# A chunked retention block with a mixture of experts: the first step in another order, and transposes on VectorE through a DRAM copy from the eleventh chunk on

## The chip, the cores and the metric

The kernel runs on one core of a Trainium2 chip. The metric is the device time of one execution in microseconds; the kernel before has a median of 623.9 us in three runs (622.66 to 626.26). Durations and starts below come from one profiled execution of it.

## What is computed

The input x is [2, 2048, 256] in float32. A layernorm without scale, then a retention layer, and the result is added to x; a second layernorm, then a mixture of 8 experts of which each token takes 2, and this too is added. Cut to what matters here:

```python
y  = layernorm(x)
v  = y @ W_write.T                       # 4 heads of 64
wk = y shifted by one token              # the first one is zero
# chunk by chunk, with a state W per head:
inter = W @ rk * g_p                     # rk: the tokens y of the chunk
S     = rk @ wk.T ;  intra = (S * M) @ v
W     = g_C * W + (v * g_w).T @ wk
x1 = x + y + (alpha * (inter + intra)) @ W_read.T
out = x1 + sum over the top 2 of 8 experts of  p_e * (gelu(layernorm(x1) @ w1_e + b1_e) @ w2_e + b2_e)
```

M, g_p, g_w and g_C are powers of a decay gamma = sigmoid(decay), made at the start from its logarithm.

## The kernel before

**Tiling.** The 2048 positions are cut into 16 chunks (`p`, 0 to 15) of P = 128 tokens, and both batch rows (b = 0, 1) of a chunk are done together, so that a tile of tokens is 128 partitions x 2 x 256. Four groups of chunks are routed to the experts as they become ready. Routed tokens are gathered per expert into tiles of at most 256 tokens, and the expert work of a tile is cut into 8 `piece`s of 128 of the 1024 hidden units (L872): a matmul group `ph` (L894), the GELU on ScalarE to `hT` (L899), and three pieces later the matmuls `py` (L850). After the eighth piece VectorE makes `yo` (L861) and GpSimd adds the rows to the output in DRAM (L864).

**One chunk.** `norm_stats` (L286) takes mean and variance on VectorE; `rstd_of` (L243) raises the variance to the power -0.5 on GpSimd (L247). `norm` (L298) writes the normed tokens `y`: on VectorE for chunks 0, 1 and from 11 on, on ScalarE for the others. Still in `norm`, three DMAs make `wk`, which is y moved down by one partition: row 0 from the last row of the chunk before (L323), then 112 rows (L324) and 15 rows (L325). Then x of the chunk p+2 is asked for. `transposes` (L349) turns y into `yT` (features on partitions, with a column ahead for the token before): four TensorE transposes into the PSUM tile `pt` (L355), one copy out of it, on VectorE for chunk 0 (L358) and on ScalarE for the others (L361). `scaled_reads` (L364) multiplies yT by g_p to `rg`, `scaled_writes` (L373) multiplies wk by g_w to `wkg`, on ScalarE for chunks below 9 and on VectorE after (L382).

`attention(p)` (L418) is a generator; between its yields the main loop places pieces of the experts. In its order: the matmuls `pv` (v, L428), the scores `pS` (L437), the masked scores `A` on VectorE (L443), `scaled_writes(p)`, the output product of the chunk before (`result`, pO, L406), `transposes(p + 1)`, from chunk 9 on `norm_stats(p + 2)`, the gate (`gate_parts`, L340), then `pR` (L480, L488), its copy `rdT` (L493), `pW` (L508), the new `state` on VectorE (L513), `scaled_reads(p + 1)` and `norm(p + 2)`.

**What sets the order.** All five engines run in the order in which the code issues (`manual_schedule`, L101); no scheduler moves anything. Nearly all loads and stores go through SyncE's (SP's) one queue, among them the experts' weights `w1c` (1 MB each, L777), the gathered tokens `xg` (L791) and their extra columns `wn` (L797). A DMA that has to wait for its source holds back all that are issued behind it in that queue. The few loads that ScalarE issues are in the first lines (L111 to L115). PSUM tiles come from pools: tag `pm` has three buffers, which ph, pv, pW and the late pO take in turn; `ps_t` has one (pt), `ps_s` one (pS and pR), `ps_y` two. So a ph waits until the third `pm` tile ahead of it has been read. SBUF tiles with tag `y` have three buffers, `wk`, `yT` and `v` two.

**The first step.** L109 to L118 ask for x of chunk 0 in two halves (SP the first, ScalarE the second, after `dec`), the write weights and the gate weights. ScalarE makes |decay|, its exponential, alpha and the logarithm (L140 to L145). The generator `decays` (L147) is run in three parts by `next(start)`: `neg` (L149); then `lg` (L151), `g_w`, and on ScalarE the masks `dmask`, g_w, g_c and g_p; then on GpSimd the causal cut of `dmask` (L162). The start order stands at L918 to L933: warm-up matmuls, `norm_stats(0)`, `norm(0)`, the second part of `decays`, the correction of the gate weights in `wwg` (L927), `transposes(0)`, a part of the set-up, the third part of `decays`, `norm_stats(1)`, `norm(1)`.

**Constants.** EASY = 9: from this chunk on VectorE takes over some of ScalarE's work. BUSY = 8: from here on chunks run among the experts' pieces. The main loop is at L979.

Of the kernel before, what the change touches and what calls it, by code (L numbers as in the profile page):

```python
# [10 lines left out]
F32 = mybir.dt.float32  # L11
I32 = mybir.dt.int32
AF = mybir.ActivationFunctionType
ALU = mybir.AluOpType
# [4 lines left out]
P = 128  # L19
B, T, D = 2, 2048, 256  # L20
# [3 lines left out]
NC = T // P  # L24
# [6 lines left out]
S = 32  # L31
Q = P // S
# [28 lines left out]
def block_kernel(  # L61
# [12 lines left out]
    b2: bass.AP,  # L74
    out: bass.AP,
    slots: bass.AP,
):
    nc = tc.nc

# [2 lines left out]
    chk = ctx.enter_context(tc.tile_pool(name="chk", bufs=2))  # L82
# [7 lines left out]
    def one(shape, dt, name):  # L90
        return keep.tile(shape, dt, name=name)
# [4 lines left out]
    def load_x(p):  # L96
        xin = chk.tile([P, B, D], F32, tag="xin", name=f"xin_{p}", bufs=4)
        nc.sync.dma_start(xin, x.rearrange("b t d -> t b d")[p * P : (p + 1) * P])
        return xin
# [8 lines left out]
    wr_sb = one([P, 2, D], F32, "wr_sb")  # L108
    xins = {0: chk.tile([P, B, D], F32, tag="xin", name="xin_0", bufs=4)}  # L109
    nc.sync.dma_start(xins[0][:, 0, :], x[0, 0:P, :])  # L110
    nc.scalar.dma_start(dec, decay)  # L111
    nc.scalar.dma_start(xins[0][:, 1, :], x[1, 0:P, :])
    nc.sync.dma_start(wwg[:, :, :D], wwT.rearrange("(c p) o -> p c o", p=P))
    nc.scalar.dma_start(wwg[:, :, D:], gateT.rearrange("(c p) e -> p c e", p=P))
    nc.scalar.dma_start(lal, log_alpha)  # L115
# [25 lines left out]
    lg = one([P, 6], F32, "lg")  # L141
    nc.scalar.activation(lg, mag, AF.Exp, scale=-1.0)
    alpha = one([P, 2], F32, "alpha")
    nc.scalar.activation(alpha, lal, AF.Exp)
    nc.scalar.activation(lg, lg, AF.Ln, bias=1.0)  # L145

    def decays():  # L147

# [21 lines left out]
    g_w = one([P, H], F32, "g_w")  # L170
# [99 lines left out]
                return  # L270

    ys, wks, yTs, x1s, ups, stats2, rgs, wkgs = {}, {}, {}, {}, {}, {}, {}, {}
    shifts, vs, rdTs = {}, {}, {}
    EASY = 9
    BUSY = 8
    LATE = 7
    mark = {}
# [2 lines left out]
    def group_tiles(q):  # L280
        if q not in x1s:
            x1s[q] = grp.tile([P, G, D + E], F32, tag="x1", name=f"x1_{q}")
            stats2[q] = grp.tile([P, G, 2], F32, tag="mv2", name=f"mv2_{q}")
        return x1s[q], stats2[q]

    def norm_stats(p):  # L286
        xin = xins[p]
        st = sml.tile([P, B, 6], F32, tag="st", name=f"st_{p}")
        mv = sml.tile([P, B, 2], F32, tag="mv", name=f"mv_{p}", bufs=3)
        for b in range(B):  # L290
            nc.vector.bn_stats(st[:, b, :], xin[:, b, :])
        for b in range(B):
            beside()
            nc.vector.bn_aggr(mv[:, b, :], st[:, b, :])
        beside()
        ups[p] = (mv, *rstd_of(mv[:, :, 1], B, f"a{p}"))

    def norm(p):  # L298

        xin = xins[p]  # L300
        mv, ve, rstd = ups[p]
        shift = shift_of(mv[:, :, 0], rstd, B, f"a{p}")
        ups[p] = (mv, ve, rstd)
        beside()
        up = sml.tile([P, B], F32, tag="up", name=f"up_{p}")
        nc.vector.tensor_scalar(up, rstd, 1.0, None, ALU.add)
        shifts[p] = (shift, up)
        y = chk.tile([P, B, D], F32, tag="y", name=f"y_{p}", bufs=3)
        for b in range(B):
            if 1 < p < EASY + 2:  # L310
                nc.scalar.activation(
                    y[:, b, :], xin[:, b, :], AF.Identity, bias=shift[:, b : b + 1], scale=rstd[:, b : b + 1]
                )
            else:
                nc.vector.tensor_scalar(
                    y[:, b, :], xin[:, b, :], rstd[:, b : b + 1], shift[:, b : b + 1], ALU.mult, ALU.add
                )

        wk = chk.tile([P, B, D], F32, tag="wk", name=f"wk_{p}")
        if p == 0:  # L320
            nc.gpsimd.memset(wk[0:1, :, :], 0.0)
        else:
            nc.sync.dma_start(wk[0:1, :, :], ys[p - 1][127:128, :, :])  # L323
        nc.sync.dma_start(wk[1:113, :, :], y[0:112, :, :])  # L324
        nc.sync.dma_start(wk[113:128, :, :], y[112:127, :, :])  # L325
        ys[p], wks[p] = y, wk
        if p + 2 < NC:
            xins[p + 2] = load_x(p + 2)

    def sums(p):  # L330

# [17 lines left out]
    def transposes(p):  # L349

        yT = chk.tile([P, B, 2, P + 1], F32, tag="yT", name=f"yT_{p}")
        pt = ps_t.tile([P, B, 2, P], F32, tag="pt", name=f"pt_{p}")
        for b in range(B):
            for c in range(2):
                nc.tensor.transpose(pt[:, b, c, :], ys[p][:, b, c * P : (c + 1) * P], ident)  # L355
        if p == 0:
            nc.gpsimd.memset(yT[:, :, :, 0:1], 0.0)
            nc.vector.tensor_copy(yT[:, :, :, 1:], pt)  # L358
        else:
            nc.scalar.copy(yT[:, :, :, 0:1], yTs[p - 1][:, :, :, P : P + 1])  # L360
            nc.scalar.copy(yT[:, :, :, 1:], pt)  # L361
        yTs[p] = yT

    def scaled_reads(p):  # L364

# [7 lines left out]
    def scaled_writes(p):  # L373
        if p < NC - 1:
            wkg = chk.tile([P, B, H, HD], F32, tag="wkg", name=f"wkg_{p}", bufs=1)
            wk = wks[p].rearrange("p b (h d) -> p b h d", h=H)
            if p < EASY:
                for h in range(H):
                    nc.scalar.activation(wkg[:, :, h], wk[:, :, h], AF.Identity, scale=g_w[:, h : h + 1])
            else:  # L380
                for b in range(B):
                    nc.vector.tensor_tensor(  # L382
                        wkg[:, b], wk[:, b], g_w.unsqueeze(2).to_broadcast([P, H, HD]), ALU.mult
                    )
            wkgs[p] = wkg
# [32 lines left out]
    def attention(p):  # L418


        q, at = p // 2, 2 * (p % 2)
        first, last = p == 0, p == NC - 1
        x1, _ = group_tiles(q)
        yT = yTs[p]
        for b in range(B):
# [21 lines left out]
        beside()  # L447
        if p + 2 < NC and p < EASY:
            norm_stats(p + 2)
# [9 lines left out]
        if not last:  # L459
            transposes(p + 1)  # L460
        if p + 2 < NC and p >= EASY:
            norm_stats(p + 2)
# [11 lines left out]
        for b in range(B):  # L474
            if first:
                break
            for hh in range(2):
                for j in range(2):
# [3 lines left out]
                        start=(b == 0), stop=False,  # L482
                    )
        for b in range(B):
            for hh in range(2):
                for j in range(2):
                    hs = slice((2 * hh + j) * HD, (2 * hh + j + 1) * HD)
# [9 lines left out]
        for b in range(B):  # L497
            if p < EASY:
                nc.scalar.activation(x1[:, at + b, D:], vs[b][:, D:], AF.Identity, scale=std1[:, b : b + 1])
            else:  # L500
                nc.vector.tensor_scalar(x1[:, at + b, D:], vs[b][:, D:], std1[:, b : b + 1], None, ALU.mult)
        if not last:
            pW = ps_m.tile([P, B, 2, HD], F32, tag="pm", name=f"pW_{p}")
            for b in range(B):
                for hh in range(2):
                    for j in range(2):
                        h = 2 * hh + j
# [34 lines left out]
    def route(q):  # L542


        early = 2 * q + 2 < BUSY
        x1, mv2 = x1s[q], stats2[q]
# [363 lines left out]
    start = decays()  # L910
# [12 lines left out]
    norm_stats(0)  # L923
    next(start)
    norm(0)
    next(start)
    nc.vector.scalar_tensor_tensor(wwg[:, :, D:], by_e(ps, 2), -1.0 / D, wwg[:, :, D:], ALU.mult, ALU.add)  # L927
    transposes(0)
    setup = setup_rest()
    next(setup)  # L930
    next(start)
    norm_stats(1)
    norm(1)  # L933

    def behind_first():
# [43 lines left out]
    for p in range(NC):  # L979
        for k, _ in enumerate(attention(p)):  # L980
            if p == 0 and k == 0:
                behind_first()
            if (p or k > 3) and k in (0, 2, 3, 4, 5) and halves < W2_BY[p]:
                e, j = divmod(halves, 2)
# [9 lines left out]
            if p < BUSY or not todo:  # L994
                advance(p > EASY)
            ask_weights_on(stream["piece"] // FC + 2)
# [79 lines left out]
```

## Time and profile before

| what | value |
|---|---|
| median of three runs | 623.9 us (622.66 to 626.26) |
| the profiled execution, its own time | 626.45 us |
| its span in the trace | 624.7 us |
| TensorE weight loads, busy | 529.3 us (85%), they overlap the matmuls |
| GpSimd, busy | 223.6 us (36%) |
| TensorE busy, 0 to 14 us / 14 to 94 / 94 to 265 / 265 to the end | 10.7 of 14 / 69.9 of 80 / 169.2 of 171 / 353.1 of 359.7 |
| VectorE busy in the same stretches | 6.2 / 63.8 / 88.7 / 90.7 us |
| share of the DMA engines in the same stretches | 0.45 / 0.84 / 0.61 / 0.60 |
| expert matmuls ph (L894) and py (L850) | 294.3 and 288.8 us |
| copy of pt to yT on ScalarE (L361) | 15 x 585 ns, from 14.6 to 246.2 us |
| rg from yT (L368, VectorE) | 15 x 684 ns |

The lines ahead of the costliest groups tell the same: two lines of expert matmuls make up most of TensorE's time, and TensorE stands idle before `ph` 5.7 us in all, of which 4.8 us are one wait at the first expert tile (89.6 to 94.4 us). The chunks' own work (attention) runs from the start to about 270 us; after that only expert tiles are left. In a line of the timeline the columns are start, duration, engine, code line, operation, out<-in, the count, and in brackets the idle time of the engine just before it with what ended it. "SPq" is SyncE's DMA queue; its durations are those of the issue, not of the transfer.

### The profile page before, as it was taken

What the parts mean: (1) busy time and instruction counts of PE and PEld (TensorE: products, weight loads), DVE (VectorE), ACT (ScalarE), POOL (GpSimd) and SP (SyncE); (2) the same over time, 40 slices, a digit from 0 to 9 for tenths busy, and PEclk for the clock granted to TensorE, in tenths of its full rate; (3) what the DMA queues carried; (4) which work ended last, traced back from release to release, by engine and by line L of the source; (5) the groups of instructions that cost most, each with busy time, mean ns of one, the idle gap of its engine ahead of it and who ended that gap; (6) DMA issues with size and microseconds to landing.
All of it is one profiled execution on the core that took longest, in us unless ns stands there. A gap on an engine that the chain in (4) does not pass through costs nothing. (4 is left out here: it accounts for less than half of the span.)

```text
span 624.7 us, 12845 instructions
## 1 busy us (share of the span) xinstructions
PE 603.0 (97%) x3864; PEld 529.3 (85%) x3864; DVE 249.3 (40%) x1039; ACT 240.7 (39%) x586; POOL 223.6 (36%) x199
## 2 busy tenths in 40 slices
PE   7998879999999999999999999999999999999995
PEld 6876758888888888888888888888888899999995
DVE  4787876567345534452255111221111132222220
ACT  6686673352333332422232222222222234444442
POOL 3216655546315622455266222222222121221121
PEclk9998998999999999999999999999999999999999
DMA  4799595679645366446657676466445568777742
GB/s 133 232 341 325 161 278 158 167 213 247 163 109 131 89 149 149 110 115 168 141 122 196 158 180 134 93 130 127 118 101 136 140 182 206 194 199 227 208 107 28
DMA packets 88856, 102.53 MB, mean 164 GB/s; under 512 B 52576, under 2 KB 77024, under 8 KB 83152
## 3 DMA queue, kind: packets, MB, share of 16 engines
q1 hardware_dynamic: 75360, 84.03, 46.8%
q0 software_dynamic: 12720, 17.47, 15.3%
q8 instruction: 35, 0.57, 0.4%
q14 instruction: 37, 0.30, 0.2%
q10 hardware_dynamic: 704, 0.14, 0.1%
HBM read 74.41 MB, written 23.01 MB: 156 GB/s over the span
## 5 line engine op out<-in xcount | busy, mean ns | idle before, releaser
L894 PE MATMUL ph<-xT,w1c 128*128 128x256 f32 (+1 forms) x1408 | 294.3, 332 | 5.7 <-issue 4.8
L850 PE MATMUL py<-w_sb,hT 128*128 x1072 | 288.8, 380 | 0.0
L899 ACT ACTIVATE hT<-ph,b1c 128x256 f32<-128x256 f32 (+1 forms) x352 | 148.4, 422 | 322.3 <-PE ph L894 293.6
L894 PEld LDWEIGHTS ph<-xT,w1c 128*128 128x128 f32 x1408 | 240.6, 192 | 34.6 <-issue 5.1
L864 POOL DMA_INDIRECT out<-yo,dest x67 | 105.2, 1570 | 291.1 <-DVE yo L861 196.1
L850 PEld LDWEIGHTS py<-w_sb,hT 128*128 128x128 f32 x1072 | 191.3, 191 | 19.2
L861 DVE SCALAR_TENSOR_TENSOR yo<-py,wt,b2c 128x256 f32<-128x256 f32 x67 | 30.3, 481 | 249.9 <-PE py L850 249.9
L536 POOL DMA_INDIRECT slots<-pay,slot_i x64 | 63.3, 989 | 62.2 <-issue 30.6
L428 PE MATMUL pv<-wwg,yT 128*128 128x264 f32 x128 | 33.9, 411 | 1.5 <-DVE yT L358 1.5
L406 PE MATMUL pO<-wrg,rdT 128*128 128x264 f32 x128 | 34.2, 401 | 0.0
L443 DVE TENSOR_TENSOR A<-pS,dmask 128x1024 f32<-128x1024 f32 x16 | 19.6, 1223 | 35.9 <-PE pS L437 28.8
L428 PEld LDWEIGHTS pv<-wwg,yT 128*128 128x128 f32 x128 | 24.4, 198 | 5.9 <-DVE yT L358 1.7
L406 PEld LDWEIGHTS pO<-wrg,rdT 128*128 128x128 f32 x128 | 24.0, 194 | 4.6 <-ACT v L430 0.2
L821 DVE STREAM_TRANSPOSE xT<-xg 128x512 f32<-128x512 f32 (+1 forms) x44 | 25.4, 576 | 0.2 <-issue 0.2
L836 DVE TENSOR_SCALAR b2c<-b2c,wt 128x256 f32<-128x256 f32 x67 | 23.8, 356 | 2.4
L409 DVE TENSOR_TENSOR x<-x,pO 128x264 f32<-128x264 f32 x32 | 13.4, 426 | 20.2 <-PE pO L406 20.2
L488 PE MATMUL pR<-A,v 128*64 128x128 f32 x256 | 18.0, 279 | 2.9 <-issue 2.2
L247 POOL TENSOR_TENSOR rstd_a<-ve_a,expo 128x2 f32<-128x2 f32 x16 | 11.6, 723 | 25.2 <-DVE ve_a L245 13.7
L566 ACT ACTIVATE pay<-x,shift_b,rstd_b 128x256 f32<-128x256 f32 x32 | 19.0, 593 | 3.8 <-DVE shift_b L252 3.7
L437 PEld LDWEIGHTS pS<-yT 64*128 64x128 f32 x256 | 15.5, 187 | 5.8 <-issue 3.7
L488 PEld LDWEIGHTS pR<-A,v 128*64 128x64 f32 x256 | 13.9, 136 | 6.0 <-issue 4.9
L437 PE MATMUL pS<-yT 64*128 64x128 f32 x256 | 18.6, 284 | 0.0
(161 smaller groups left out, 392.5 us busy)
## 6 DMA issues: line engine op xcount, KB each, us to landing
w1c<-in_w SPq DMA_DIRECT2D x44, 1024.0 KB
w_sb<-in_w SPq DMA_DIRECT2D x16, 512.0 KB
xg<-slots SPq DMA_DIRECT2D x92, 64.0 KB
b2c<-in_b SPq DMA_DIRECT2D x44, 128.0 KB
out<-x SPq DMA_DIRECT2D x16, 256.0 KB
xin<-in_x SPq DMA_DIRECT2D x15, 256.0 KB
wk<-y SPq DMA_DIRECT2D x16, 224.0 KB
xg<-slots SPq DMA_DIRECT2D x84, 32.0 KB
```

The source lines that it names most:

```text
L406: nc.tensor.matmul(pO, lhsT=rdTs[p][:, c, b * P : (b + 1) * P], rhs=wrg[:, c, :], start=(c == 0), stop=(c == 1))
L428: nc.tensor.matmul(pv, lhsT=yT[:, b, c, 1:], rhs=wwg[:, c, :], start=(c == 0), stop=(c == 1))
L437: nc.tensor.matmul(pS[:, j, (2 * b + hh) * P : (2 * b + hh + 1) * P], lhsT=yT[r, b, hh, 0:P], rhs=yT[r, b, hh, 1:], start=True, stop=True,)
L488: nc.tensor.matmul(pR[half(j, hh), hh, b * P : (b + 1) * P], lhsT=vs[b][:, hs], rhs=A[:, j, b, hh * P : (hh + 1) * P], start=(first and b ...
L536: put = nc.gpsimd.indirect_dma_start(out=next(slot_views), out_offset=IndirectOffsetOnAxis(ap=index, axis=0), in_=rows, in_offset=None,)
L821: nc.vector.transpose(xT.rearrange("p c (i s) -> p c i s", s=S), xg.rearrange("p i (c s) -> p c i s", s=S))
L836: nc.vector.tensor_scalar(b2c[:, j], b2c[:, 0], wt[:, j : j + 1], None, ALU.mult)
L850: nc.tensor.matmul(r["py"][:, j * D : (j + 1) * D], lhsT=hT[:, j * SB : (j + 1) * SB], rhs=w2_sb[:, ds(r["at"], 1), fc * D : (fc + 1) * D] ...
L861: nc.vector.scalar_tensor_tensor(yo, r["py"][:, j * D : (j + 1) * D], r["wt"][:, j : j + 1], r["b2c"][:, j], ALU.mult, ALU.add)
L864: add = nc.gpsimd.indirect_dma_start(out=next(out_views), out_offset=IndirectOffsetOnAxis(ap=r["dest"][:, j : j + 1], axis=0), in_=yo, in_ ...
L894: nc.tensor.matmul(ph, lhsT=r["w1c"][:, c, fc * P : (fc + 1) * P], rhs=r["xT"][:, c, :], start=(c == 0), stop=(c == 1),)
L899: mark[0] = nc.scalar.activation(hT, ph, AF.Gelu_apprx_tanh, bias=r["b1c"][:, fc : fc + 1]).ins.name
```

## The change

It has two parts.

The first step is put in another order. ScalarE asks for the second half of x before `dec`. The logarithm comes before the exponential that makes alpha. For chunk 0 the small operation `up` is issued after y instead of before it, the copy of pt to yT is cut into two halves with the second part of `decays` (lg, g_w, masks) between them, and the correction of the gate weights comes before that part. The statistics of chunk 1, with GpSimd's power at their end, are issued before the third part of `decays`, the causal cut on GpSimd.

From chunk 10 on (SQUARE = 10) the normed tokens go through a new DRAM tensor `normed` [16, 256, 256]. `norm` writes y with its columns in another order (32-column squares with the two 128-halves beside each other) and stores it with one DMA, in place of the three DMAs of wk. At the start of `attention(p)` a new function `squares(p + 1)` issues on SP's queue: wk rows 1 to 127 from `normed` in one DMA, row 0 from the chunk before (for chunk 10 four small DMAs from the old y in SBUF), and four DMAs that read the tokens as `yg`, a tile of 32-token squares in which each quarter of the partitions holds one group of 32 columns; `yg` takes a buffer of the tag `y`. `transposes(p)` then is one small ScalarE copy and two VectorE stream transposes of 128 x 256 from yg to yT, in place of the four TensorE transposes, pt and the ScalarE copy of 128 x 512. `scaled_writes` reads wk by squares, in four 128 x 128 products instead of two of 128 x 256.

```diff
@@ -74,6 +74,7 @@
     b2: bass.AP,
     out: bass.AP,
     slots: bass.AP,
+    normed: bass.AP,
 ):
     nc = tc.nc
 
@@ -108,8 +109,8 @@
     wr_sb = one([P, 2, D], F32, "wr_sb")
     xins = {0: chk.tile([P, B, D], F32, tag="xin", name="xin_0", bufs=4)}
     nc.sync.dma_start(xins[0][:, 0, :], x[0, 0:P, :])
+    nc.scalar.dma_start(xins[0][:, 1, :], x[1, 0:P, :])
     nc.scalar.dma_start(dec, decay)
-    nc.scalar.dma_start(xins[0][:, 1, :], x[1, 0:P, :])
     nc.sync.dma_start(wwg[:, :, :D], wwT.rearrange("(c p) o -> p c o", p=P))
     nc.scalar.dma_start(wwg[:, :, D:], gateT.rearrange("(c p) e -> p c e", p=P))
     nc.scalar.dma_start(lal, log_alpha)
@@ -141,8 +142,8 @@
     lg = one([P, 6], F32, "lg")
     nc.scalar.activation(lg, mag, AF.Exp, scale=-1.0)
     alpha = one([P, 2], F32, "alpha")
+    nc.scalar.activation(lg, lg, AF.Ln, bias=1.0)
     nc.scalar.activation(alpha, lal, AF.Exp)
-    nc.scalar.activation(lg, lg, AF.Ln, bias=1.0)
 
     def decays():
 
@@ -270,8 +271,9 @@
                 return
 
     ys, wks, yTs, x1s, ups, stats2, rgs, wkgs = {}, {}, {}, {}, {}, {}, {}, {}
-    shifts, vs, rdTs = {}, {}, {}
+    shifts, vs, rdTs, ygs = {}, {}, {}, {}
     EASY = 9
+    SQUARE = 10
     BUSY = 8
     LATE = 7
     mark = {}
@@ -303,19 +305,28 @@
         ups[p] = (mv, ve, rstd)
         beside()
         up = sml.tile([P, B], F32, tag="up", name=f"up_{p}")
-        nc.vector.tensor_scalar(up, rstd, 1.0, None, ALU.add)
         shifts[p] = (shift, up)
+        if p:
+            nc.vector.tensor_scalar(up, rstd, 1.0, None, ALU.add)
         y = chk.tile([P, B, D], F32, tag="y", name=f"y_{p}", bufs=3)
         for b in range(B):
+            at = by_square(y[:, b]) if p >= SQUARE else y[:, b]
+            of = xin[:, b].rearrange("p (c k s) -> p c k s", c=2, s=S) if p >= SQUARE else xin[:, b]
             if 1 < p < EASY + 2:
                 nc.scalar.activation(
-                    y[:, b, :], xin[:, b, :], AF.Identity, bias=shift[:, b : b + 1], scale=rstd[:, b : b + 1]
+                    at, of, AF.Identity, bias=shift[:, b : b + 1], scale=rstd[:, b : b + 1]
                 )
             else:
                 nc.vector.tensor_scalar(
-                    y[:, b, :], xin[:, b, :], rstd[:, b : b + 1], shift[:, b : b + 1], ALU.mult, ALU.add
+                    at, of, rstd[:, b : b + 1], shift[:, b : b + 1], ALU.mult, ALU.add
                 )
-
+        if p == 0:
+            nc.vector.tensor_scalar(up, rstd, 1.0, None, ALU.add)
+
+        ys[p] = y
+        if p >= SQUARE:
+            nc.sync.dma_start(normed[p].rearrange("(b t) d -> t b d", b=B), y)
+            return next_x(p)
         wk = chk.tile([P, B, D], F32, tag="wk", name=f"wk_{p}")
         if p == 0:
             nc.gpsimd.memset(wk[0:1, :, :], 0.0)
@@ -323,9 +334,37 @@
             nc.sync.dma_start(wk[0:1, :, :], ys[p - 1][127:128, :, :])
         nc.sync.dma_start(wk[1:113, :, :], y[0:112, :, :])
         nc.sync.dma_start(wk[113:128, :, :], y[112:127, :, :])
-        ys[p], wks[p] = y, wk
+        wks[p] = wk
+        next_x(p)
+
+    def next_x(p):
         if p + 2 < NC:
             xins[p + 2] = load_x(p + 2)
+
+    def by_square(t):
+
+        return t.rearrange("p (k c s) -> p c k s", c=2, s=S)
+
+    def squares(p):
+
+
+        wk = chk.tile([P, B, D], F32, tag="wk", name=f"wk_{p}")
+        nc.sync.dma_start(wk[1:P], normed[p].rearrange("(b t) d -> t b d", b=B)[: P - 1])
+        if p > SQUARE:
+            nc.sync.dma_start(wk[0:1], normed[p - 1].rearrange("(b t) d -> t b d", b=B)[P - 1 : P])
+        else:
+            for b in range(B):
+                for c in range(2):
+                    nc.sync.dma_start(
+                        by_square(wk[0:1, b])[:, c],
+                        ys[p - 1][P - 1 : P, b, c * P : (c + 1) * P].rearrange("p (k s) -> p k s", s=S),
+                    )
+        wks[p] = wk
+        yg = chk.tile([P, B * Q, 2, S], F32, tag="y", name=f"yg_{p}", bufs=3)
+        rows = normed[p].rearrange("(j s) (k d) -> s j k d", s=S, k=Q)
+        for k in range(Q):
+            nc.sync.dma_start(yg[k * S : (k + 1) * S].rearrange("p j c s -> p j (c s)"), rows[:, :, k, :])
+        ygs[p] = yg
 
     def sums(p):
 
@@ -349,17 +388,29 @@
     def transposes(p):
 
         yT = chk.tile([P, B, 2, P + 1], F32, tag="yT", name=f"yT_{p}")
+        yTs[p] = yT
+        if p >= SQUARE:
+            nc.scalar.copy(yT[:, :, :, 0:1], yTs[p - 1][:, :, :, P : P + 1])
+            yg = ygs.pop(p)
+            for b in range(B):
+                nc.vector.transpose(
+                    yT[:, b, :, 1:].rearrange("p c (i s) -> p c i s", s=S),
+                    yg[:, b * Q : (b + 1) * Q].rearrange("p i c s -> p c i s"),
+                )
+            return
         pt = ps_t.tile([P, B, 2, P], F32, tag="pt", name=f"pt_{p}")
         for b in range(B):
             for c in range(2):
                 nc.tensor.transpose(pt[:, b, c, :], ys[p][:, b, c * P : (c + 1) * P], ident)
         if p == 0:
+
             nc.gpsimd.memset(yT[:, :, :, 0:1], 0.0)
-            nc.vector.tensor_copy(yT[:, :, :, 1:], pt)
+            nc.vector.tensor_copy(yT[:, 0, :, 1:], pt[:, 0])
+            next(start)
+            nc.vector.tensor_copy(yT[:, 1, :, 1:], pt[:, 1])
         else:
             nc.scalar.copy(yT[:, :, :, 0:1], yTs[p - 1][:, :, :, P : P + 1])
             nc.scalar.copy(yT[:, :, :, 1:], pt)
-        yTs[p] = yT
 
     def scaled_reads(p):
 
@@ -377,6 +428,15 @@
             if p < EASY:
                 for h in range(H):
                     nc.scalar.activation(wkg[:, :, h], wk[:, :, h], AF.Identity, scale=g_w[:, h : h + 1])
+            elif p >= SQUARE:
+                for b in range(B):
+                    for c in range(2):
+                        hs = slice(2 * c, 2 * c + 2)
+                        nc.vector.tensor_tensor(
+                            wkg[:, b, hs].rearrange("p h (k s) -> p h k s", s=S),
+                            by_square(wks[p][:, b])[:, c].rearrange("p (h k) s -> p h k s", h=2),
+                            g_w[:, hs].unsqueeze(2).unsqueeze(3).to_broadcast([P, 2, 2, S]), ALU.mult,
+                        )
             else:
                 for b in range(B):
                     nc.vector.tensor_tensor(
@@ -420,6 +480,8 @@
 
         q, at = p // 2, 2 * (p % 2)
         first, last = p == 0, p == NC - 1
+        if SQUARE <= p + 1 < NC:
+            squares(p + 1)
         x1, _ = group_tiles(q)
         yT = yTs[p]
         for b in range(B):
@@ -923,13 +985,12 @@
     norm_stats(0)
     next(start)
     norm(0)
-    next(start)
     nc.vector.scalar_tensor_tensor(wwg[:, :, D:], by_e(ps, 2), -1.0 / D, wwg[:, :, D:], ALU.mult, ALU.add)
     transposes(0)
     setup = setup_rest()
     next(setup)
+    norm_stats(1)
     next(start)
-    norm_stats(1)
     norm(1)
 
     def behind_first():
@@ -1069,7 +1130,8 @@
         args.append(nc.dram_tensor(f"in_{name}", a.shape, mybir.dt.from_np(a.dtype), kind="ExternalInput").ap())
     out = nc.dram_tensor("out_0", (N + SB, D), F32, kind="ExternalOutput").ap()
     slots = nc.dram_tensor("slots", (DUMMY + SB, ROW), F32, kind="Internal").ap()
+    normed = nc.dram_tensor("normed", (NC, B * P, D), F32, kind="Internal").ap()
     with tile.TileContext(nc) as tc:
-        block_kernel(tc, *args, out, slots)
+        block_kernel(tc, *args, out, slots, normed)
     r = run_bass_kernel_spmd(nc, [arrays], core_ids=[0])
     return r.results[0]["out_0"][:N].reshape(B, T, D)
```

The built program has 24 TensorE instructions fewer than before; on VectorE the yT transposes of chunk p+1 stand where the statistics of chunk p+2 began, with these behind them.

## The prediction

> **What bounds the kernel now.** I read the busy shares first, then busy time by stretches, then TensorE's timeline around one transpose group, then the timeline of the first 14 us, then SP and VectorE around chunk 11.
>
> ```profile
> PE 603.0 (97%) x3864; PEld 529.3 (85%) x3864; DVE 249.3 (40%) x1039; ACT 240.7 (39%) x586; POOL 223.6 (36%) x199
> ...
> PE   7998879999999999999999999999999999999995
> ...
> DMA  4799595679645366446657676466445568777742
> ```
>
> TensorE is the bound from the seventh slice on: 9 in every slice to the last, while VectorE is at 40%. Before that (0 to 94 us) the chunks are a chain of latencies. So TensorE work removed after 100 us is gained in full, a TensorE wait added there is lost in full, and work beside TensorE costs nothing until TensorE waits for it.
>
> ```profile
> 210.39 0.60 PE L355 MATMUL pt<-ident,y 128*128 128x128 f32 x4
> 210.83 1.03 PE L894 MATMUL ph<-xT,w1c 128*128 128x256 f32 x4
> ```
>
> From start to start the four transposes of chunk 14 hold TensorE for 210.83 - 210.39 = 0.44 us; the same 0.44 stands at 126.69 and 179.93. Their 0.60 us is latency, and overlaps what follows.
>
> ```profile
> 6.80 1.28 ACT L145 ACT_TABLE_LOAD   x1
> ...
> 8.33 0.17 DVE L151 SCALAR_TENSOR_TENSOR lg<-lg,neg 128x6 f32<-128x6 f32 x1 [0.81 <-ACT lg L145]
> ...
> 9.49 2.05 PE L428 MATMUL pv<-wwg,yT 128*128 128x264 f32 x8 [1.48 <-DVE yT L358]
> ...
> 11.82 0.73 POOL L247 TENSOR_TENSOR rstd_a<-ve_a,expo 128x2 f32<-128x2 f32 x1
> ...
> 13.43 1.22 DVE L443 TENSOR_TENSOR A<-pS,dmask 128x1024 f32<-128x1024 f32 x1
> ```
>
> At the start VectorE waits 0.81 us for the logarithm, whose table load waited behind `alpha`; the yT copy and TensorE wait behind that; chunk 1's power on GpSimd starts after the mask (11.22 to 11.85), and A (13.43) stands behind chunk 1's y on VectorE.
>
> **First step: a gain of 2.3 us.** The logarithm's table load can follow `lg` at 4.54: lg at 6.03 instead of 8.30, so VectorE's 0.81 us wait goes. The second half of x is asked for 0.44 us earlier (slot 0.82 for 1.26; it ended a 1.11 us wait at 4.52), worth 0.44 to 1.1; `dec` comes as much later, and is needed only at 4.09, behind the first table load. Walking VectorE's rows on: y ends near 7.0, first half copy by 7.7, lg and g_w 8.0, second half 8.3, statistics of chunk 1 end 9.5 (10.52 before), power 9.6 to 10.3 ahead of the mask, y of chunk 1 by 11.3, A at 11.3. ACT's masks start near 7.8 instead of 9.88. A gains 2.1, ACT 2.1, and ACT had 0.75 us in hand before `rdT`. 2.3 is taken; the bounds are 0.8 (only the wait) and 3. All later work up to 94 us hangs on this chain, so it carries. Three small VectorE operations moved behind y cost nothing: their readers come later.
>
> **Transposes: a gain of 2.6 us.** Six chunks (10 to 15) x 0.44 = 2.6. Six copies of 585 ns (L361) also leave ACT, which waits for TensorE anyway: nothing. VectorE gets two 128x256 stream transposes per chunk (436 ns each in L821's row: 0.87 us), and four 128x128 products instead of two of 418 ns (between 0 and 0.8 us more; 0.3 by its near rows). VectorE waits between its work there (4.38 us before A at 120.96), so without the data's lateness this is free; without that cover it would be 1.2 us for each chunk, 7 in all.
>
> **The new wait.** The yT transposes stand in VectorE's order where chunk p+1's statistics stand now. Behind them are these statistics, the gate, and `state` (L513), which frees the PSUM buffer of pW. TensorE's third ph after pW takes that buffer.
>
> ```profile
> 127.92 0.74 DVE L291 BATCH_NORM_STATS2 st<-xin 128x6 f32<-128x256 f32 x2
> ...
> 132.06 0.61 DVE L513 SCALAR_TENSOR_TENSOR state<-state,g_c,pW 128x128 f32<-128x128 f32 x2 [2.11 <-PE pW L508]
> ```
> ```profile
> 111.27 0.68 PE L894 MATMUL ph<-xT,w1c 128*128 128x128 f32 x4 [0.29 <-PE py L850]
> ...
> 133.81 0.61 PE L894 MATMUL ph<-xT,w1c 128*128 128x128 f32 x4
> ```
>
> For chunk 11 the VectorE work from 127.92 to the gate's end at 129.95 is 2.03 us; with 0.87 for the transposes and 0.7 for `state`, yg must have landed by 133.81 - 3.6 = 130.2. For chunk 10 the wall is 111.27 (work 105.60 to 108.46 = 2.86): 106.9. For chunk 12 it is 159.44 (work 3.46): 154.5; for 13 about 182.5, for 14 and 15 216 and 252.
>
> When does it land? SP's order in the built program shows it:
>
> ```profile
> ...
> 112.61 0.53 SPq L324 DMA_DIRECT2D wk<-y  x1
> ...
> 122.27 0.47 SPq L777 DMA_DIRECT2D w1c<-in_w  x1
> ...
> 126.08 1.77 SPq L797 DMA_DIRECT2D wn<-slots  x1
> ...
> ```
>
> SP's waits from 129 to 134 us (sum, count, mean), and the stretch of chunk 11 by engines, with clock, DMA share and GB/s at its end:
>
> ```profile
> SPq L324 <- DMA w1c<-in_w: 1.8, 1, 1.8
> ```
> ```profile
> 124.00:132.00 8.00, 8.00 (x88) 7.02 (x87) 4.29 (x24) 3.66 (x10) 3.35 (x3) 1.00 1.02 332
> ```
>
> SP works without rest from y of chunk 11 (112.6) on; wk_11 and yg_11 come only behind wn of tile 4, at 127.9, less 1.05 since one `normed` write replaces two wk writes: 126.8. SP's DMAs take eight completion semaphores in turn, each waiting for the one eight before it: yg_11's first read thus waits for tile 4's 1 MB w1c, which by the wait of 1.8 us from 129.5 landed at 131.3, now 130.3. Four reads at 0.5 us and 2.2 us to land (the first x: issued 0.82, read 2.98) give 134.5. That is 4.3 us too late whatever else holds.
>
> **The rule that speaks against it.** The Trainium skill, DMA: Bandwidth & Descriptors, section "Why a DMA increments its semaphore by 16 and not by 1", says that a DMA from SP runs on the largest number of engines up to 16 that divides the slowest dimension of both sides, and names 127 partitions as a case of one engine. The old code moves wk as 112 + 15 rows (seven per engine, one per engine); the new one as 127 rows of 2 KB, ahead of yg in the same queue. By the same page ("Queues, rings and completion order") each engine takes its queue's packets in order, so that one engine's part of yg stands behind all of them. No row of this trace shows a single-engine transfer, so I bound it. By the row of 31 to 47 us (341 GB/s, share 1.03) one engine moves 341/16 = 21 GB/s: 260 KB take 12.2 us; by the 27 GiB/s per engine of the same page's section "Specifications" (an estimate) 9.0. I take 11, nearer the row, since most of it falls where the engines are full. yg's own part on that engine is 64 packets at 62 ns (46.8% x 16 x 624.7 / 75360) = 4 us.
> - Chunk 10: SP reaches wk at 98.5 less 1.65 (y_10's two wk writes and its row gone) = 96.9. It lands at 96.9 + 1.7 + 11 = 109.6; the fourth yg read shares its semaphore and waits for it: 109.6 + 2.2 = 111.8 against 106.9: 4.9 us lost.
> - Chunk 11: that engine clear at 130.3, + 11 + 4 = 145.3 against 130.2: 15.1.
> - Chunk 12: w1c of tile 6 keeps the engines full to about 153 (share 1.04 over 146 to 154), an us earlier now: 152 + 15 = 167 against 154.5: 12.5.
> - Chunk 13: 168 + 15 = 183 against 182.5: 0 to 1. Chunks 14 and 15 have room.
> Without the rule the sum is 4.3 (chunk 11 alone); with it 32.5. Tile loads later in SP's queue have two tiles in hand.
>
> After each of these waits TensorE's clock counts too. The row nearest is the old 4.8 us wait at 94.4, with a granted clock of 0.63 over 94 to 102: pO took 1.97 instead of 1.05 us, two ph groups 2.0 instead of 1.2: 2.5 us. Bounds 0 and 2.7 for each of three waits; I take 1.5 each, 4.5 in all.
>
> **Sum.** -2.3 - 2.6 + 32.5 + 4.5 = +32.1 us. The profiled execution took 626.45 us, its span 624.7; the runs' median is 623.9. The difference is put on the median: 656.0 us. Its own range: engine at 9.0 us -6, clock 0 -4.5; engine at 12.2 +3.6, clock 2.7 each +3.6: 645 to 664.
>
> **Rivals.**
> 1. The 127 rows spread over many engines. For it: only the page, no row, says otherwise. Against: the old split into 112 and 15. Then only w1c's landing counts: 623.9 - 4.9 + 4.3 = 623.3, to 626 with the clock.
> 2. Not slower but faster: yg lands in time. Its place is SP's queue between y_11 and wk_11 (112.6 to 126.8) and the w1c landing at 130.3. It decides if yg_11 lands before 130.2 and yg_10 before 106.9, say because w1c's transfers clear four us sooner with two wk writes and `out` behind them. Then all waits are covered: 623.9 - 4.9 = 619.0. For it: wk_10 leaves 1.65 us earlier and the DMA share over 94 to 102 is only 0.49. Against: 3.5 MB move between 118 and 132, with the share at 1.02 from 124.
> 3. The start's gain does not carry (DMA full from 31 to 62 us): 2.3 us more in each case.
>
> **How the numbers follow.** The measurement tells about 0.5% (3.1 us) from no change. One engine for wk, slower: 0.57. Rival 1: 0.18, nearly all within 0.5%. Rival 2: 0.20, faster. The rest 0.05, spread. Faster 0.22 (rival 2 and the low end of rival 1), same 0.17, slower 0.61. Both signs hold weight, so the range reaches from 617.5, under rival 2's value by half of the start's uncertainty, to 665; it leaves out about 0.08 at either side. The likeliest case's own range is 645 to 664.
>
> **What would show it.** The transposes of chunks 10, 11 and 12 on VectorE with idle time of 5, 15 and 13 us before them, ended by DMA yg; TensorE idle at the third ph after pW(9), pW(10), pW(11); 24 fewer L355 records; A of chunk 0 near 11.3; a granted clock below 1 after each wait. I am wrong if VectorE reaches those transposes and starts at once, if only chunk 11 waits (rival 1), or if A of chunk 0 stays at 13.

## Result and the profile after

The changed kernel takes 656.7 us (median of four runs, 655.79 to 658.9), beside 624.25 us for four runs of the kernel before on the same chip: 1.052 times as long, 95% interval 1.048 to 1.056. Its profiled execution took 655.79 us, with a span of 654.1 us for 624.7. The forecast was 656.0 us. The total and its main cause held; several terms of the sum did not, and their errors cancelled.

The page's busy times and three of its rows in 40 slices:

```profile
PE 608.3 (93%) x3840; PEld 531.7 (81%) x3840; DVE 255.4 (39%) x1062; ACT 236.5 (36%) x580; POOL 224.6 (34%) x199
...
PE   8998878747998799999999999999999999999995
...
PEclk9999999786999799999999999999999999999999
DMA  3799671954645744674665676536644568878752
```

TensorE has 24 instructions less and yet 5.3 us more of busy time, so it ran slower; its idle time rose from 21.7 to 45.8 us. Both stand in the slices 7 to 14, about 100 to 225 us, and nowhere later. (Line numbers are those of each kernel: ph is L956 here, the transposes on VectorE L396, `state` L575.) TensorE's timeline, those of its waits after 85 us that are above 1 us, and that of chunk 12:

```profile
90.54 1.13 PE L956 MATMUL ph<-xT,w1c 128*128 128x128 f32 x8 [1.83 <-DVE xT L883]
...
95.30 1.16 PE L466 MATMUL pO<-wrg,rdT 128*128 128x264 f32 x4 [1.41 <-ACT hT L961]
...
112.65 3.71 PE L490 MATMUL pv<-wwg,yT 128*128 128x264 f32 x8 [2.66 <-DVE yT L396]
...
121.92 1.19 PE L956 MATMUL ph<-xT,w1c 128*128 128x128 f32 x4 [4.47 <-DMA w1c<-in_w]
...
151.61 1.19 PE L956 MATMUL ph<-xT,w1c 128*128 128x128 f32 x4 [13.42 <-DVE state L575]
...
186.29 2.02 PE L490 MATMUL pv<-wwg,yT 128*128 128x264 f32 x8 [0.34 <-DVE yT L396]
...
217.44 2.04 PE L956 MATMUL ph<-xT,w1c 128*128 128x256 f32 x4 [7.10 <-DVE state L575]
```

VectorE's timeline shows what `state` stood behind, the transposes of chunks 10 to 13:

```profile
112.06 0.77 DVE L396 STREAM_TRANSPOSE yT<-yg 128x256 f32<-128x256 f32 x2 [10.78 <-DMA yg<-normed]
...
148.26 0.77 DVE L396 STREAM_TRANSPOSE yT<-yg 128x256 f32<-128x256 f32 x2 [15.70 <-DMA yg<-normed]
...
185.69 0.77 DVE L396 STREAM_TRANSPOSE yT<-yg 128x256 f32<-128x256 f32 x2 [13.22 <-DMA yg<-normed]
...
214.21 0.77 DVE L396 STREAM_TRANSPOSE yT<-yg 128x256 f32<-128x256 f32 x2 [14.97 <-DMA yg<-normed]
```

Four times VectorE stands still for 11 to 16 us, until yg has landed. The transposes themselves take 0.77 us for each chunk, a little less than the 0.87 forecast. SP's timeline shows when yg is asked for (chunk 11; start, then duration of the issue):

```profile
133.18 0.35 SPq L352 DMA_DIRECT2D wk<-normed  x1
133.59 8.17 SPq L354 DMA_DIRECT2D wk<-normed  x1
141.80 2.02 SPq L366 DMA_DIRECT2D yg<-normed  x4
```

The DMA of 127 rows (L352) is issued in 0.35 us. The next, one row of 2 KB, stops SP for 8.17 us, and yg is asked for only then. In the chunks from 11 on this issue took 7.3 to 11.5 us. And VectorE can start only 4.4 us after the last of the four issues of yg (143.82 to 148.26). What the DMA engines do meanwhile stands in two stretches, with clock, DMA share and GB/s at the end:

```profile
138.00:141.80 3.80, 0.19 (x1) 0.00 (x0) 0.00 (x0) 0.00 (x0) 0.00 (x0) 1.00 0.07 23
146.00:148.20 2.20, 0.00 (x0) 0.00 (x0) 0.00 (x0) 0.00 (x0) 0.00 (x0) 0.50 0.07 21
```

A share of 0.07 is one engine of sixteen (1/16 = 0.0625). The trace's list of single transfers says the same: the rows of wk go one after another, 1 KB every 44 ns, for 11.2 us until 146.76 (row 0 as the last), and directly behind them, until 147.69, go 64 transfers of yg, its part on that engine. So in this chunk, and in chunk 12 alike, the rows ahead of yg on the one engine set when yg lands; the stop of SP delays, besides, whatever is asked for behind.

### The profile page after: what moved, and what is told of

The parts are those of the page before. It is cut to its first block, busy times and chain, and to the rows that moved or that the text cites. A ratio compares the mean times of both kernels' runs of the same rounds, so it can differ in the third digit from the quotient of the medians.

```text
span 654.1 us, 12853 instructions
## 1 busy us (share of the span) xinstructions
PE 608.3 (93%) x3840; PEld 531.7 (81%) x3840; DVE 255.4 (39%) x1062; ACT 236.5 (36%) x580; POOL 224.6 (34%) x199
## 3 DMA queue, kind: packets, MB, share of 16 engines
q1 hardware_dynamic: 83962, 87.18, 45.8%
## 5 line engine op out<-in xcount | busy, mean ns | idle before, releaser
L956 PE MATMUL ph<-xT,w1c 128*128 128x256 f32 (+1 forms) x1408 | 296.7, 334 | 27.5 <-DVE state L575 20.5
L912 PE MATMUL py<-w_sb,hT 128*128 x1072 | 291.9, 383 | 0.0
L956 PEld LDWEIGHTS ph<-xT,w1c 128*128 128x128 f32 x1408 | 242.6, 193 | 58.3 <-issue 28.5
L396 DVE STREAM_TRANSPOSE yT<-yg 128x256 f32<-128x256 f32 x12 | 4.6, 425 | 61.2 <-DMA yg<-normed 61.2
L898 DVE TENSOR_SCALAR b2c<-b2c,wt 128x256 f32<-128x256 f32 x67 | 25.4, 380 | 2.6 <-DMA xg<-slots 0.3
L469 DVE TENSOR_TENSOR x<-x,pO 128x264 f32<-128x264 f32 x32 | 13.3, 425 | 19.3 <-PE pO L466 18.3
L499 PEld LDWEIGHTS pS<-yT 64*128 64x128 f32 x256 | 15.5, 187 | 5.9 <-issue 3.8
```

Source lines behind the costliest of these rows:

```text
L499: nc.tensor.matmul(pS[:, j, (2 * b + hh) * P : (2 * b + hh + 1) * P], lhsT=yT[r, b, hh, 0:P], rhs=yT[r, b, hh, 1:], start=True, stop=True,)
L898: nc.vector.tensor_scalar(b2c[:, j], b2c[:, 0], wt[:, j : j + 1], None, ALU.mult)
L912: nc.tensor.matmul(r["py"][:, j * D : (j + 1) * D], lhsT=hT[:, j * SB : (j + 1) * SB], rhs=w2_sb[:, ds(r["at"], 1), fc * D : (fc + 1) * D] ...
L956: nc.tensor.matmul(ph, lhsT=r["w1c"][:, c, fc * P : (fc + 1) * P], rhs=r["xT"][:, c, :], start=(c == 0), stop=(c == 1),)
```

## The experiments

Each ratio is to the kernel before in the same session, with its 95% interval. The kernel before took 620.1 to 620.2 us in the first two sessions and 625.0 to 625.5 us in the last two.

**127 rows in two DMAs (wk_split).**

```diff
-nc.sync.dma_start(wk[1:P], normed[p].rearrange("(b t) d -> t b d", b=B)[: P - 1])
+nc.sync.dma_start(wk[1:113], normed[p].rearrange("(b t) d -> t b d", b=B)[:112])
+nc.sync.dma_start(wk[113:P], normed[p].rearrange("(b t) d -> t b d", b=B)[112 : P - 1])
```

> The changed kernel, but rows 1 to 127 of wk are read from normed in two DMAs, of 112 and 15 rows, as the kernel before did from y. Theory (127 rows go through one DMA engine, and hold up what is behind them in SP's queue): the DMA issued next on SP's queue takes about 0.6 us again instead of 7.3 to 11.5, VectorE waits at most 5 us ahead of the yT transposes of chunks 11 and 12 and not at all from 13 on, and the time is 620 to 627 us. Rival (the trip through DRAM behind the weights in SP's order is late by itself): waits of 10 us and more ahead of the transposes of chunks 10 to 13 stay, and the time stays above 645 us.

Measured: 628.5 us, 1.014 (1.011 to 1.017). Three quarters of the loss are gone, but more remains than the theory allowed (620 to 627 us). SP's timeline of this kernel for chunk 11:

```profile
123.48 0.55 SPq L352 DMA_DIRECT2D wk<-normed  x1
124.49 0.37 SPq L353 DMA_DIRECT2D wk<-normed  x1
127.58 0.65 SPq L355 DMA_DIRECT2D wk<-normed  x1
128.27 2.90 SPq L367 DMA_DIRECT2D yg<-normed  x4
```

The single row now takes 0.65 us, and yg lands within 1.6 us of its last issue. But SP reaches these reads at 123.5, behind the asks of three tiles, and the row waits 2.7 us for w1c ahead of it. VectorE still waits in chunks 11, 12 and 13 (10.9, 6.3 and 2.9 us); TensorE's largest wait left is behind the first of them, beside 1.6 us for a w1c:

```profile
132.77 0.77 DVE L397 STREAM_TRANSPOSE yT<-yg 128x256 f32<-128x256 f32 x2 [10.87 <-DMA yg<-normed]
```
```profile
136.12 1.19 PE L957 MATMUL ph<-xT,w1c 128*128 128x128 f32 x4 [7.46 <-DVE state L576]
```

This is the mechanism of the prediction's first rival, at 7.5 us for 4.3: chunk 11 waits though no DMA of 127 rows is left.

**113 and 14 rows (wk_113)**, the same edit with another cut.

> As the version with wk read in 112 and 15 rows, but in 113 and 14 rows: 113 is a prime number, like 127, and 112 is not. Theory (the count of rows decides on how many DMA engines they lie, and a count with no divisor up to 16 lies on one): the issues behind the DMA of 113 rows are held up for 6.5 to 10 us (113/127 of the 7.3 to 11.5 us), VectorE waits 10 us and more ahead of the yT transposes of chunks 11 to 13, and the time is within 6 us of the changed kernel's, 1.04 to 1.06 of before. Rival (it is the size of the one DMA or its length in rows, and cutting it up is what helped): as with 112 and 15 rows, 1.010 to 1.018 of before, with no hold of more than 3 us on SP's queue.

Measured: 648.6 us in two runs, 1.046 (1.044 to 1.049). The issue behind the 113 rows is held again:

```profile
130.00 0.34 SPq L352 DMA_DIRECT2D wk<-normed  x1
130.39 6.50 SPq L353 DMA_DIRECT2D wk<-normed  x1
```

Over the six chunks it took 6.2 to 11.4 us, with 112 rows 0.4 to 1.0. VectorE's waits for yg are back (7.7, 13.9, 12.5 and 14.8 us in chunks 10 to 13), and within the hold, from 134.5 to 136.9 us, the DMA share is 0.07 again. One row more makes the difference, so it is the count's divisors and not the size, as the Trainium skill says of 127 partitions (DMA: Bandwidth & Descriptors, section "Why a DMA increments its semaphore by 16 and not by 1"). That such rows lie on one engine the share of 0.07 shows; why SP stops behind them no run here shows.

**yg ahead of wk (yg_first)**: in `squares`, the four reads of yg are issued before those of wk, the 127 rows as they were.

> The changed kernel, but squares asks for yg before wk, still 127 rows in one DMA. Theory (one engine, and the queue stopped behind it): VectorE's waits ahead of the yT transposes fall to at most 6 us for chunks 11 and 12, the 7 to 11 us now fall on row 0 of wk and so on what follows it in SP's queue (out, the next x, the next tile's tokens), which is partly covered: 625 to 640 us. Rival (the landing of yg is late because of SP's order and of the eight semaphores): no change by more than 4 us, about 655.

Measured: 632.7 us, 1.018 (1.015 to 1.022): as the theory has it. VectorE's waits for yg fall to 6.1 and 6.7 us in chunks 11 and 12, a little over the 6 expected, and end there; the hold moves to what is behind wk, and TensorE's largest wait is now 8.57 us for a tile's w1c at 123.38.

**Reads behind the write (early)**: wk_split, with `squares(p)` called in `norm(p)` after the next x.

```diff
+            next_x(p)
+            squares(p)
+            return
...
-        if SQUARE <= p + 1 < NC:
-            squares(p + 1)
```

> wk in 112 and 15 rows, and the reads of normed (wk, yg) are asked for directly behind its write and the next x, in norm(p), not at the start of attention(p). Theory (what is left of the loss in that version, 8.3 us, is SP's order: the reads of chunk 11 stand behind the asks of three tiles and wait for w1c): the wait of 10.9 us on VectorE ahead of the yT transposes of chunk 11 and the 7.5 us on TensorE at the third ph after pW(10) go, no wait of more than 1 us on TensorE replaces them, and the time falls to before less the 2.6 us of TensorE's transposes, 0.993 to 0.999 of it. Rival (the wait of the reads for the write's landing, some 2 us on SP's queue in each chunk, holds up the tiles' asks): TensorE waits at the first ph of a tile for w1c or xg, and 1.003 to 1.012.

Measured: 629.6 us, 1.016 (1.014 to 1.018): the rival, somewhat above its range. VectorE's wait ahead of the transposes of chunk 11 is gone, but it waits for the tiles' tokens instead; TensorE waits 6.8 us for a VectorE instruction behind the second of these waits (at 131.83):

```profile
101.54 0.45 DVE L884 STREAM_TRANSPOSE xT<-xg 128x256 f32<-128x256 f32 x1 [7.06 <-DMA xg<-slots]
...
125.07 0.45 DVE L884 STREAM_TRANSPOSE xT<-xg 128x256 f32<-128x256 f32 x1 [4.78 <-DMA xg<-slots]
```

SP waited 5.9 us there for `normed` to land (two waits, up to 3.5 us).

**Another queue (on_act)**: wk_split, with every DMA of `squares` as `nc.scalar.dma_start`.

> wk in 112 and 15 rows, at the old place in the order, but the reads of normed are issued from ScalarE's queue and not from SP's. Theory (what is left of the loss is SP's queue between 90 and 130 us, which has no room for eight to ten more DMAs: they wait behind the tiles' asks, or the tiles' asks behind them): VectorE waits under 2 us ahead of the yT transposes of chunks 10 to 12, TensorE has no wait over 1 us after the first tile's ph, and the time falls to before less the 2.6 us of TensorE's transposes, 0.993 to 0.999 of it. Rival 1 (the DMA engines, full with w1c, are the limit, whoever asks): as with SP, waits of 6 us and more for yg in chunk 11, 1.010 to 1.018. Rival 2 (4 us of issuing per chunk on ScalarE hold up v, hT and rdT): TensorE waits for ACT instead, 1.000 to 1.010.

Measured: 645.9 us, 1.033 (1.028 to 1.038), worse than rival 2 had it; the six runs spread from 638.8 to 648.8 us, and the profile is of the fastest. ScalarE's timeline, then TensorE's:

```profile
101.18 0.66 ACT L493 COPY v<-pv 128x264 f32<-128x264 f32 x2 [11.16 <-DMA xg<-slots]
```
```profile
101.61 1.22 PE L957 MATMUL ph<-xT,w1c 128*128 128x128 f32 x4 [9.26 <-ACT v L493]
```

Of these 11.2 us ScalarE spends about 5 issuing the ten DMAs. The rest are waits between them for DMAs in flight, first for the write to `normed`, last for SP's xg as the trace infers it; v, and TensorE with it, wait. VectorE's only wait for yg in these chunks is 0.85 us, so rival 1's wait of 6 us and more does not appear, though VectorE itself came later here.

**Only where SP has room (split_13, trip_13, best)**: wk_split with SQUARE = 13; the same with the first step as before; the same with the first step in the new order but `lg` ahead of the copies.

> wk in 112 and 15 rows on SP's queue, but the trip through DRAM only for chunks 13, 14 and 15 (SQUARE = 13), where SP and the DMA engines have room. Theory: no wait on VectorE ahead of the yT transposes, no wait on TensorE, three chunks x 0.44 us = 1.3 us gained, 0.996 to 1.000 of before. Rival (VectorE's transposes cost TensorE something even with yg in time, by contention or in the order behind them): 1.001 to 1.006.

> The first step as before; the trip through DRAM for chunks 13 to 15 alone, wk in 112 and 15 rows. Theory (the gain of the version with SQUARE = 13, 0.9958, comes from TensorE's three transpose groups): 0.996 to 0.999 of before, and no wait on TensorE after 130 us. Rival (it comes from the first step's new order): 0.999 to 1.002.

> The trip for chunks 13 to 15 with wk in 112 and 15 rows, and the first step's new order with lg ahead of the copies of yT. Theory (the first step adds nothing that can be measured, its gain ends in the stretch of full DMA engines): the same as with SQUARE = 13, 0.995 to 0.998. Rival (both parts gain, and their gains add up): 0.991 to 0.994.

Measured: split_13 622.7 us, 0.9958 (0.994 to 0.998); trip_13 623.5 us, 0.9965 (0.994 to 0.999); best 621.3 us, 0.9948 (0.992 to 0.998). All three are faster than the kernel before by 0.35 to 0.52%, and no interval reaches 1. In split_13 VectorE starts the transposes of chunk 13 without a wait, and TensorE has no wait from 130 us on:

```profile
176.00 0.77 DVE L397 STREAM_TRANSPOSE yT<-yg 128x256 f32<-128x256 f32 x2
```

So with the data in time the edit gains. The 1.3 us of three transpose groups (0.9979 as a ratio) lie inside the interval of trip_13 and just outside those of the other two. Whether the first step adds to it these three can't tell apart: their intervals overlap.

**The parts by themselves (squares_only, start_only, lg_first, after_again).** squares_only leaves the first step as before; start_only has SQUARE = 16; lg_first is start_only with one line moved; after_again is the changed kernel.

```diff
+            next(start)
             nc.vector.tensor_copy(yT[:, 0, :, 1:], pt[:, 0])
-            next(start)
             nc.vector.tensor_copy(yT[:, 1, :, 1:], pt[:, 1])
```

> Only the trip through DRAM from chunk 10 on, with the first step as before. Theory: all of the loss lies here, 655 to 660 us, with the waits of the yT transposes as in the changed kernel. Rival (part of the loss comes from the late start): below 653 us.

> Only the first step's new order; no chunk goes through DRAM (SQUARE = 16). If the late start in the changed kernel's profile (A of chunk 0 at 14.59 us for 13.43, with the first TensorE instructions at 350 ns for 256) belongs to the new order, A of chunk 0 is again near 14.6; if it was chance, A is near 11.3. For the time: forecast of record 623.9 - 2.3 = 621.6 us; rival (the stretch of 30 to 60 us, with the DMA engines full, swallows what the start gives or takes): 623 to 625.

> Only the first step's new order, with one thing put back: lg, g_w and the masks are issued on VectorE before the first half copy of yT, not between the two halves. Theory (in the new order lg stands on VectorE behind the first half copy, this behind pt, and pt behind warm-up matmuls that run slowly in some executions, so that the masks start late): lg at 7.0 to 7.8 us instead of 10.6, dmask on ScalarE near 8 to 9, A of chunk 0 at 11.3 to 13, set by pt alone. Rival (pt and TensorE set A whatever is done on VectorE): A stays at 14.5 to 15.5. For the time both say that the stretch of full DMA engines from 30 to 60 us swallows it: 0.998 to 1.001 of before.

> The changed kernel unchanged, on the chip of these runs, whose time for the kernel before is 620.1 us and not 624.3. Theory: the ratio does not hang on the chip, 1.048 to 1.056, and so the first step's order adds nothing to the loss of the trip through DRAM (1.0586 by itself) and may take 0.5% off it. Rival (it does, and the difference between the two ratios is the chip's): 1.056 to 1.062, the same as with the trip alone.

Measured: squares_only 655.8 us, 1.059 (1.055 to 1.062), the whole loss. start_only 620.2 us, 1.0006 (0.9986 to 1.0026); lg_first 619.7 us, 0.9997 (0.9982 to 1.0011): nothing either way. after_again 654.9 us, 1.048 (1.045 to 1.051); its ratio is below that of squares_only, but they were not in one session and their times differ by 0.9 us, so a gain of the first step beside the trip is neither shown nor excluded.

The expectations of start_only and lg_first said that the stretch of full DMA engines swallows what the start gives. Seven profiles speak against that. Start of pt, of A of chunk 0, and of the first expert matmul in the profiles of the first two sessions, from their timelines:

| kernel | pt | A of chunk 0 | first ph | first ph less A |
|---|---|---|---|---|
| early | 6.78 | 11.69 | 89.20 | 77.5 |
| wk_113 | 7.08 | 12.00 | 89.62 | 77.6 |
| wk_split | 7.62 | 12.54 | 90.11 | 77.6 |
| squares_only (old order) | 7.37 | 12.79 | 89.68 | 76.9 |
| lg_first | 8.40 | 12.98 | 91.39 | 78.4 |
| yg_first | 8.52 | 15.22 | 93.05 | 77.8 |
| start_only | 8.47 | 15.54 | 93.52 | 78.0 |

In these seven, by as much as A is late the first expert matmul is late too, within 0.8 us: here the start carries. In the other seven it is not seen, the difference runs from 75.9 to 82.1 us; best has its A 0.8 us later than trip_13 and its first ph 3.6 us earlier. So whether the start carries stays open. What is plain is that A itself gains nothing on average: over nine profiles of the new order it stands between 11.7 and 15.5 (mean 13.2), over three of the old one at 12.8, 13.3 and 13.4 (mean 13.2).

## Why the forecast came out, point by point

**The one-engine DMA: right, and shown.** wk_split takes most of the loss away, wk_113 brings it back, and the DMA share in the hold is that of one engine. The size of the rows was well taken: 11.2 us in chunk 11 for 11 forecast, between its bounds of 9.0 and 12.2. The first rests on the 27 GiB/s of the Trainium skill (DMA: Bandwidth & Descriptors, section "Specifications"); the 23 GB/s measured here are less, and the trace's row (21 GB/s) was nearer. yg's own part on that engine was not: 0.9 us for 4, since its transfers of 256 bytes took 14 ns each there and not the mean of 62 ns. In chunk 11 yg still landed 3 us later than forecast, since the rows began on the engine at 135.5 and not at 130.3. One thing was missing: the forecast let SP go on behind that DMA; in fact SP itself stops, for 7.3 to 11.5 us.

**The sum of the waits: right in total, wrong in its terms.** Forecast were 4.9, 15.1, 12.5 and up to 1 us for chunks 10 to 13, 32.5 in all, and nothing for the tiles. TensorE waited 2.7, 13.4, 1.1 (0.34 and 0.72) and 7.1 us, and 4.5 us for a tile's w1c: 28.7.
- Chunk 11 is right, behind the third ph after pW(10): 13.4 us for 15.1.
- Chunks 10 and 12: the step "TensorE's third ph after pW takes that buffer" failed. VectorE was as late as expected, 10.8 and 13.2 us. But in the changed program's order the third ph there does not wait for `state`; TensorE runs six pieces after pW(11), from 175.32 to 185.9, and waits only at pv, for yT itself. For the transposes of chunk 13 it is the fourth ph after pW(12) (204.33) that waits, at 217.44. The edit changes which of the three `pm` buffers a tile gets: in the built programs the buffers of pW(9) and pW(11) go to the third ph behind them before the edit, but only to a ph behind the next pv after it. The forecast took the order of the kernel before. (The third ph behind pW(11) stands at 159.54 there; the forecast's 159.44 is a slip, its 154.5 comes from the former.)
- Chunk 13: "0 to 1" failed, 15.0 us on VectorE and 7.1 on TensorE. The forecast had SP at these reads 14.5 us ahead of the time they were needed (168 to 182.5). SP had been held until 178.9 in the chunk before, and reached them at 199.65, 10.7 us before TensorE stopped at 210.34; then it was held 7.3 us more.
- "Tile loads later in SP's queue have two tiles in hand" failed: SP was held on the rows of chunk 10 (issues from 96.12 to 105.80), and the next tile's w1c, asked for at 103.07 before, is asked for at 115.03; TensorE waits for it 4.5 us, until 121.92.

**The clock: right in kind, too small.** A stretch of the kernel before, then four of the changed kernel, with the granted clock third from the end:

```profile
116.00:133.00 17.00, 16.44 (x145) 14.12 (x144) 8.62 (x35) 6.54 (x17) 7.22 (x7) 1.00 0.84 233
...
105.00:116.00 11.00, 8.34 (x40) 6.35 (x38) 3.73 (x19) 2.71 (x8) 1.75 (x2) 0.86 0.23 51
116.00:133.00 17.00, 12.53 (x73) 10.84 (x72) 10.06 (x42) 3.19 (x10) 10.30 (x10) 0.79 1.01 299
133.00:150.00 17.00, 5.19 (x67) 4.16 (x66) 1.70 (x8) 0.58 (x2) 0.00 (x0) 0.81 0.36 97
150.00:170.00 20.00, 18.39 (x94) 16.16 (x95) 14.37 (x62) 8.30 (x20) 11.80 (x7) 0.82 0.70 157
```

In the kernel before the clock is 1.00 from 105 us to the last few us. In the changed kernel the trace's list of granted clocks has half speed for 3.4, 4.6, 5.6 and 4.6 us after the ends of the waits of 2.7, 4.5, 13.4 and 7.1 us: 18 us at half speed, which by estimate cost 9 us, against a forecast of 4.5. Net it is less, since the kernel before loses some too, after its wait at the first tile: TensorE's busy time is 608.3 us for 603.0 less the 2.6 of the transposes, 7.9 us of slower work, of which 1.0 lies ahead of the first expert tile.

**The transposes: right.** 24 instructions less; trip_13's gain fits the 1.3 us of its three groups, and no cost of VectorE's transposes shows where yg is in time.

**The first step: wrong.** 2.3 us were forecast; start_only shows no gain. The step that failed is "first half copy by 7.7". In the changed kernel's start:

```profile
7.36 2.05 PE L978 MATMUL warm<-ident 128*128 128x128 f32 x8
...
9.21 1.06 PE L404 MATMUL pt<-ident,y 128*128 128x128 f32 x4
...
10.30 0.42 DVE L408 COPY yT<-pt 128x256 f32<-128x256 f32 x1 [2.59 <-PE pt L404]
10.64 0.16 DVE L152 SCALAR_TENSOR_TENSOR lg<-lg,neg 128x6 f32<-128x6 f32 x1
...
14.59 1.22 DVE L505 TENSOR_TENSOR A<-pS,dmask 128x1024 f32<-128x1024 f32 x1
```

The logarithm is ready at 6.0, as worked out, but lg now stands on VectorE behind the half copy, this behind pt, and pt on TensorE behind the eight warm-up instructions. With the logarithm off the path, TensorE is next, which the forecast did not ask. lg_first takes lg out of that place (7.70 instead of 9.91) and A still follows pt (12.98). Behind a given pt the new order does gain: A comes 4.9 us after pt in six of its nine profiles, and 5.4 to 6.3 us after it in the old order. But pt itself starts anywhere between 6.8 and 9.2 us. `ps` ahead of it starts at 5.4 to 7.0, and the eight warm-up instructions take 1.14 us in nine of the fourteen profiles and up to 2.05 in the others. The granted clock goes with the second: its first entry of full speed in the trace's list begins at 4.3 to 6.5 us in those nine, but at 7.5 to 14.0 us in four of the others (10.41 in the changed kernel), and the fifth, start_only, has half speed from 7.9 to 14.7. No run here controls when the clock comes, so the start's time in one execution is partly luck. That it hangs on the new order is not shown; the old order's three begin at 4.3, 6.2 and 7.5.

**Why the total fits.** From before's span: waits in chunks 10 to 13 and for w1c +28.7, slower work +7.9, transposes -2.6, the first tile's waits 3.2 for 4.8 us, 1.25 us of small waits after it gone, 1.8 us less idle time before 86 us: +29.4, which is 654.1 - 624.7. Forecast were +32.1. That the total came so near is luck in part: chunks 10 to 12 were forecast 15.4 us too high (32.5 for 17.1), chunk 13, the w1c and the clock together 15.0 too low.

## What to carry to other kernels

Count the rows of a DMA: of those tried here 112 and 15 were cheap, and the primes 113 and 127 put all rows on one engine and held the queue for 6 to 12 us. The trip through DRAM cost the transposing engine little (0.77 us for each chunk) and the queue that carries it much; put it where that queue has room, and look at what is asked for behind it. After taking one wait off a path, walk the other inputs of the same step, and read the changed program's own order for the buffer that each instruction waits for.

## What the runs showed of the hardware

- The DMA issued behind 127 rows took 7.3 to 11.5 us to issue and so held its queue, behind 112 rows 0.4 to 1.0 us. The 127 rows of 2 KB went over one DMA engine in 11.2 us, at 23 GB/s.
- Reads issued on ScalarE's queue kept ScalarE from its own work for 11.2 us, about 5 of them issuing and the rest waits for DMAs in flight, among them SP's xg as the trace infers it: in this program another queue did not make them independent.
- TensorE's first instructions run at two speeds: the four weight loads of ps take 186 to 192 ns in the profile before and 288 to 338 ns in the changed kernel's, and the trace's list of granted clocks begins, with full speed, at 4.33 and 10.41 us. A stretch's mean counts the time ahead of the first entry as 1.00, and so does not show it.
